# Layer 1's keys and queries by seven block products in place of eight, in a two-layer attention kernel

## The chip, the cores and the metric

The kernel runs on one core of one Trainium2 chip. The metric is the device time of one execution in microseconds (us), lower is better. Of the kernel before there are three timed runs: 2729.54, 2733.97 and 2734.0 us, median 2733.97 us. Beside them stands one execution that was taken with the hardware profiler; every duration below comes from that one.

## What is computed

Two layers work on an image of 2 x 512 channels x 64 x 32, in f32: two batches of 2048 tokens with 512 channels. Layer 0 is an attention with 8 heads of 64, whose keys and queries take an embedding of position beside the channels. Layer 1 is a Nystroem attention with 256 landmarks (each the mean of 8 tokens) and a convolution of the values, and after it a feed-forward map. The part that the change touches is the projection of layer 1's keys and queries and what is read off them at once:

```python
qkv = x @ Wqkv                      # x: normalised tokens, (b, n, 512)
q, k, v = jnp.split(qkv, 3, axis=-1)
q, k, v = (tohead(q), tohead(k), tohead(v))
q = q * scale
qL = q.reshape(b, h, m, l, d).sum(axis=3) / l      # landmarks, l = 8
kL = k.reshape(b, h, m, l, d).sum(axis=3) / l
attn2 = jax.nn.softmax(jnp.einsum('bhid,bhjd->bhij', qL, kL), axis=-1)
```

## The kernel before, in words

Tokens of one batch are held as four blocks of 512 (`NTB = 4`, `TB = 512`); a block is a tile of 128 partitions x 4 chunks of channels x 512 tokens. The 8 heads are worked two at a time, as four **pairs** of each batch; a pair's weight for the keys (or the queries) is a tile of 128 x 4 chunks x 128 columns.

**The unit of the change.** `Pair.keys_and_queries` (from L1231) is a generator. For each of the four token blocks it makes the keys and then the queries: four matmuls (one for each chunk of channels) add up in one PSUM bank (L1244 to L1247), ScalarE copies the bank to SBUF (L1248), SyncE stores the 512 columns in DRAM (L1249), and VectorE takes the sums over 8 tokens (L1250) and the largest absolute value (L1253). That is eight **units** of four matmuls for a pair, with a `yield` after each. After the fourth block L is scaled (L1258), stored, and a few small operations make two bounds from it (L1262 to L1270).

**What stands beside the units.** The engines TensorE, VectorE, ScalarE and GpSimd run their instructions in the order in which the program writes them (`manual_schedule`); only SyncE's DMA queue is ordered by the scheduler. So the interleaving of the generators is the order of the work.

- `Pair.front` of the pair before: `attend` makes the landmark scores on PE (L1286), their exponentials on ScalarE (L1293) and the softmax on VectorE (L1297 to L1303); `gram(0)` and `gram(1)` multiply the softmax by itself (L1313: two banks each, copied out by ScalarE, L1320).
- `others(b, ...)` goes through pairs 1, 2 and 3 of a batch: one unit of the pair, then `attend` of the pair before it, two units, the two `gram`s, and the remaining five units, with a `yield` after each.
- **In batch 0** `others` is advanced by the loop over t (after `drain(out0(0))`) that also finishes layer 0 of batch 1: for each of four token blocks the output projection `out0` (four units of PE, L968, each followed by a VectorE addition, L975, that frees the bank) and the normalisation `norm0_steps`. Its steps are: sums over chunks on VectorE (L986, L987); the mean on PE (L990) and the subtraction on VectorE (L991); the squares on ScalarE (L994, L997) and their sums on VectorE (L1002, L1003); the variance on PE (L1006) and its root on ScalarE (L1008); and, a block later, called as `next(last)`, the reciprocal on VectorE (L1023), the two halves of the multiplication on GpSimd (L1025) and VectorE (L1026), and a DMA issued by GpSimd (L1027).
- **In batch 1** `others` is advanced by a plain loop, and from its eleventh step on each step is followed by one of `second_of_first` (values, landmark attention and convolution of the first pair).

The order of that first loop, for t = 0 to 3:

```python
advance(more)                    # more: others(0, ...)
next(norm)                       # mean, subtraction
advance(more_out or more)        # more_out: out0(t + 1), none at t = 3
if last is not None:
    next(last)                   # reciprocal, multiplication on GpSimd
advance(more_out or more)
next(norm)                       # squares
advance(more, 2 if advance(more_out, 2) else 4)
next(norm)                       # variance, root
```

PSUM has eight banks. In batch 0's stage two of them are the pool behind `bank(...)`, which units, `out0`, the mean, the variance and `gram` all share; `scores_bank` has four, and `values_bank` two that lie idle there. In batch 1's stage `bank(...)` has four and `product_bank` two.

Of the kernel before, what the change touches and what calls it, by code (L numbers as in the profile page):

```python
# [10 lines left out]
F32 = mybir.dt.float32  # L11
I32 = mybir.dt.int32
AF = mybir.ActivationFunctionType
ALU = mybir.AluOpType
AX = mybir.AxisListType

P = 128
B, C, H, W = 2, 512, 64, 32
S = H * W
KC = C // P  # L20
HEADS, D = 8, 64
NPAIR = HEADS // 2
TB = 512
NTB = S // TB
NST = S // P
LM, POOL = 256, S // 256
# [637 lines left out]
def fast_path(  # L664
# [35 lines left out]
    nc = tc.nc  # L700
    dram = ctx.enter_context(tc.tile_pool(name="dram1", bufs=1, space=bass.MemoryType.DRAM))
    const = ctx.enter_context(tc.tile_pool(name="const1", bufs=1))
    small = ctx.enter_context(tc.tile_pool(name="small1", bufs=2))
    banks = ExitStack()
    ps = banks.enter_context(tc.tile_pool(name="ps1", bufs=2, space=bass.MemoryType.PSUM))
    qopool = ctx.enter_context(tc.tile_pool(name="qo1", bufs=NPAIR + 1))
# [4 lines left out]
    kvpool = both.enter_context(tc.tile_pool(name="kv1", bufs=2))  # L711
# [5 lines left out]
    xh_d = dram.tile([B, C, S], F32, name="xh_fd")  # L717
    mT_d = dram.tile([P, KC, C], F32, name="mT_fd")
    k_d = dram.tile([B, NPAIR, P, S], F32, name="k_fd")
    X_d = dram.tile([B, NPAIR, 2, P, 2, LM], F32, name="X_fd")  # L720
    e_d = dram.tile([2, NPAIR, P, S], F32, name="e_fd")
    q_d = dram.tile([B, NPAIR, P, S], F32, name="q_fd")
    o_d = dram.tile([B, NPAIR, P, S], F32, name="o_fd")
    A_d = dram.tile([B, NPAIR, 2, P, 2, LM], F32, name="A_fd")
    L_d = dram.tile([B, NPAIR, P, 2, LM], F32, name="L_fd")
    band_d = dram.tile([HEADS, P * (BAND + 1)], F32, name="band_fd")

    def chunked(ap):
        return ap.rearrange("(k p) n -> p k n", p=P)

    def bank(name):
        return ps.tile([P, 512], F32, tag="pp", name=name)
# [17 lines left out]
    def exps(name):  # L750
        p = ppool.tile([P, 4 * (LM + 1)], F32, tag="p", name=name)
        return p[:, :1024].rearrange("p (h n) -> p h n", h=2)

    def block_of(pool, tag, name):
        return pool.tile([P, KC, TB], F32, tag=tag, name=name)

    def row_of(name):
        return apool.tile([P, TB], F32, tag="rinv", name=name, bufs=3)
# [48 lines left out]
    def drain(gen):  # L807
        for _ in gen:
            pass

    def gap(n=1):
        for _ in range(n):
            yield GAP

    def chain(*gens):
        for g in gens:
            yield from g
# [18 lines left out]
    def load_x(src, b, name, first=0, n=NTB):  # L836
        tiles = []
        for t in range(first, first + n):
            xb = block_of(xpool, "xb", f"{name}_{b}_{t}")
            nc.sync.dma_start(xb, chunked(src[b])[:, :, t * TB : (t + 1) * TB])  # L840
            tiles.append(xb)
        return tiles
# [16 lines left out]
    class Heads0:  # L859


        def __init__(self, b, hp, xbs):
            self.b, self.hp, self.xbs = b, hp, xbs
            self.name = f"f0_{b}_{hp}"
            self.n_units = 13 if b else 15
# [145 lines left out]
    def out0_units(b, t, xb, oTs):  # L1011

        yield from residual_units(b, t, xb, oTs, wo_sb, b0_sb, f"f0_{b}_{t}")
        nc.gpsimd.dma_start(chunked(x1_d[b])[:, :, t * TB : (t + 1) * TB], xb)
# [189 lines left out]
    def write_bands():  # L1204
# [6 lines left out]
        for h in range(HEADS):  # L1211
            nc.sync.dma_start(band_d[h].rearrange("(p q) -> p q", q=BAND + 1), rows[:, h, :])

    class Pair:


# [11 lines left out]
        def begin(self):  # L1228
            self.w = {j: self.load_w(j) for j in (1, 0)}

        def keys_and_queries(self, pool, tag, xhs, after=lambda t: None):  # L1231

            big = small.tile([P, 2, NTB], F32, tag="big", name=f"big_{self.name}", bufs=3)
            most = small.tile([P, 4], F32, tag="most", name=f"most_{self.name}", bufs=3)
            self.L = [
                lmpool.tile([P, LM], F32, tag=f"L{j}", name=f"L{j}_{self.name}") for j in range(2)
            ]
            k = kvpool.tile([P, S], F32, tag="k", name=f"k_{self.name}")
            q = pool.tile([P, S], F32, tag=tag, name=f"q_{self.name}")
            for t in range(NTB):  # L1240
                toks, marks = slice(t * TB, (t + 1) * TB), slice(t * TB // POOL, (t + 1) * TB // POOL)
                for j, dst, dst_d in ((1, k, k_d), (0, q, q_d)):
                    pp = bank(f"pp{j}_{self.name}_{t}")
                    for c in range(KC):  # L1244
                        nc.tensor.matmul(  # L1245
                            pp, lhsT=self.w[j][:, c, :], rhs=xhs[t][:, c, :], start=c == 0, stop=c == KC - 1
                        )  # L1247
                    nc.scalar.copy(dst[:, toks], pp)  # L1248
                    nc.sync.dma_start(dst_d[self.b, self.hp][:, toks], dst[:, toks])  # L1249
                    nc.vector.tensor_reduce(  # L1250
                        self.L[j][:, marks], dst[:, toks].rearrange("p (m l) -> p m l", l=POOL), AX.X, ALU.add
                    )
                    nc.vector.tensor_reduce(  # L1253
                        big[:, j, t : t + 1], dst[:, toks], AX.X, ALU.max, apply_absolute_value=True
                    )
                    if t == NTB - 1:
                        L = self.L[j]
                        nc.vector.tensor_scalar(L, L, (1.0, D**-0.5)[j == 0] / POOL, None, ALU.mult)  # L1258
                        nc.sync.dma_start(L_d[self.b, self.hp][:, j, :], L)
                    yield  # L1260
                after(t)
            nc.vector.tensor_reduce(most[:, :2], big, AX.X, ALU.max)  # L1262
            for j in range(2):
                nc.vector.tensor_reduce(
                    most[:, 2 + j : 3 + j], self.L[j], AX.X, ALU.max, apply_absolute_value=True
                )

            c = B * NPAIR + 2 * self.i
            nc.vector.tensor_tensor(bound[:, c : c + 1], most[:, 2:3], most[:, 1:2], ALU.mult)
            nc.vector.scalar_tensor_tensor(  # L1270
                bound[:, c + 1 : c + 2], most[:, :1], D**-0.5, most[:, 3:], ALU.mult, ALU.mult
            )
# [447 lines left out]
    todo = [(b, hp) for b in range(B) for hp in range(NPAIR)]  # L1720
# [4 lines left out]
    for n, (b, hp) in enumerate(todo[:-1]):  # L1725
# [5 lines left out]
        if finish is None:  # L1731
            units = nxt.units(wait=nb - b)
        else:

            units = nxt.units(False, lambda: outs_done)
# [20 lines left out]
    lmpool = both.enter_context(tc.tile_pool(name="lm1", bufs=2))  # L1756
# [4 lines left out]
    pairs = [[Pair(b, hp) for hp in range(NPAIR)] for b in range(B)]  # L1761
    xhs = load_x(xh_d, 0, "xh")
    pairs[0][0].begin()
    units = chain(gap(2), pairs[0][0].keys_and_queries(qopool, "qo", xhs))
# [3 lines left out]
    def beside(main, other):  # L1768

        for n in main:  # L1770
            yield
            for _ in range(n):
                if next(other, other) is other:
                    break
                yield

    def others(b, xhs, last, after=lambda t: None):

        for hp in range(1, NPAIR):
            pair = pairs[b][hp]  # L1780
            pair.begin()
            units = pair.keys_and_queries(kvpool, "k", xhs, after if hp + 1 == NPAIR else lambda t: None)
            next(units)
            yield
            yield from beside(last.front(), units)
            yield from units
            last = pair


    next_xhs, over = [], False  # L1790

    def load_next(t):
        assert over
        next_xhs.extend(load_x(xh_d, 1, "xh", t, 1))

    more = [others(0, xhs, pairs[0][0], load_next)]
    b = B - 1

    def as_block(tile):
# [8 lines left out]
    def norm0(t):  # L1808
        part = apool.tile([P, 2, TB], F32, tag="acc", name=f"part_f0_{t}")
        return norm0_steps(b, t, xbs_[t % 2], xns_[t % 2], part)  # L1810

    def out0(t):
        xb = xbs_[t % 2]
        nc.sync.dma_start(xb, chunked(x[b])[:, :, t * TB : (t + 1) * TB])
        return out0_units(b, t, xb, oTs)

    drain(out0(0))
    last, norm = None, norm0(0)
    next(norm)
    for t in range(NTB):  # L1820
# [12 lines left out]
        last = norm  # L1833
# [19 lines left out]

    xhs = next_xhs
    pairs[1][0].begin()
    units = pairs[1][0].keys_and_queries(kvpool, "k", xhs)
    next(units)
    drain(beside(pairs[0][-1].front(), units))
    drain(units)
    todo = pairs[1] + pairs[0]  # L1860
# [16 lines left out]
    def second_of_first():  # L1877
        pair = todo[0]
        yield from values(0)
        yield from pair.attn3()  # L1880
        landmarks, start, conv = pair.landmarks_values(), pair.start_values(), convolution(0)
        for part in (landmarks, conv, landmarks, start, conv):
            next(part)
            yield
        drain(conv)
        next(start)
        yield
# [5 lines left out]

    xhs_of = [xhs]
    first = second_of_first()
    for i, _ in enumerate(others(1, xhs, todo[0])):
        if i == 8:
            todo[0].prefetch_w()
            todo[0].prefetch()
        if i >= 10:  # L1900
            next(first, None)
# [27 lines left out]
    for n, pair in enumerate(todo):  # L1929
        before = todo[n - 1] if n else None  # L1930
        after = todo[n + 1] if n + 1 < len(todo) else None
# [18 lines left out]
        if n:  # L1950
            q = late_buffer if n > NPAIR + 1 else lambda name: kvpool.tile([P, S], F32, tag="k", name=name)
# [236 lines left out]
```

## Time and profile before

| | |
|---|---|
| timed runs | 2729.54, 2733.97, 2734.0 us (median 2733.97) |
| span of the profiled execution | 2730.4 us (its own time is not listed apart; the span lies between the lowest and the highest run, 3.6 us under the median) |
| TensorE (PE) busy | 2688.2 us, 98% of the span |
| VectorE (DVE) / ScalarE (ACT) / GpSimd (POOL) busy | 1628.1 / 903.7 / 161.8 us |
| matmuls of layer 1's keys and queries, L1245 | 512 records, 227.8 us of PE |
| stage of batch 0, 1401.9 to 1555.1 us: PE, DVE, POOL busy | 149.0, 103.3, 20.0 of 153.2 us |
| stage of batch 1, 1555.1 to 1721.3 us: PE, DVE, POOL busy | 166.2, 75.2, 0.0 of 166.2 us |

How to read it: an f32 matmul leaves two records on PE, each with a weight load of its own (PEld) that lies beside the matmul before it. The mean of one record (597 ns) is longer than the distance from one record to the next (0.43 us), because records overlap in the pipeline; the distance is what a matmul costs. A group's idle time, with the engine and line that ended it, is the time in which the engine had nothing to run just before that group. The two stages run from the end of `drain(out0(0))` to the `attend` of batch 0's last pair, and from there to that of batch 1's last pair.

### The profile page before, as it was taken

What the parts mean: (1) busy time and instruction counts of PE and PEld (TensorE: products, weight loads), DVE (VectorE), ACT (ScalarE), POOL (GpSimd) and SP (SyncE); (2) the same over time, 40 slices, a digit from 0 to 9 for tenths busy, and PEclk for the clock granted to TensorE, in tenths of its full rate; (3) what the DMA queues carried; (4) which work ended last, traced back from release to release, by engine and by line L of the source; (5) the groups of instructions that cost most, each with busy time, mean ns of one, the idle gap of its engine ahead of it and who ended that gap; (6) DMA issues with size and microseconds to landing.
All of it is one profiled execution on the core that took longest, in us unless ns stands there. A gap on an engine that the chain in (4) does not pass through costs nothing.

```text
span 2730.4 us, 41173 instructions
## 1 busy us (share of the span) xinstructions
PE 2688.2 (98%) x16994; PEld 1361.7 (50%) x16994; DVE 1628.1 (60%) x2087; ACT 903.7 (33%) x1352; POOL 161.8 (6%) x109
## 2 busy tenths in 40 slices
PE   9999999999999999999999999999999999999999
PEld 5343443434443334344344455777677666655344
DVE  3768777664557765656667544445544645465565
ACT  1434343434334334444422223223323222231210
POOL 0101101000001100000002000000000000000000
PEclk9999999999999999999999999999999999999999
DMA  4100000212111200012024632312212112121211
GB/s 147 43 10 24 28 21 24 86 36 70 32 65 56 97 24 21 24 40 77 24 89 167 207 120 93 103 33 90 79 37 63 59 44 97 34 71 42 89 39 48
DMA packets 111476, 173.99 MB, mean 64 GB/s; under 512 B 16176, under 2 KB 67888, under 8 KB 106672
## 3 DMA queue, kind: packets, MB, share of 16 engines
q1 hardware_dynamic: 105136, 150.00, 17.0%
q0 software_dynamic: 5440, 20.97, 2.1%
q8 instruction: 135, 2.21, 0.3%
q14 instruction: 61, 0.50, 0.1%
q10 hardware_dynamic: 704, 0.31, 0.0%
HBM read 90.87 MB, written 63.57 MB: 57 GB/s over the span
## 4 chain that ended last, share of the span: by engine, by line
PE 90%; DVE 5%; DMA 1%; SPq 1%; ACT 1%; issue 1%; POOL 0%; DVEq 0%; ACTq 0%; POOLq 0%
PE sc_f L1072 15%; PE av_f L1102 15%; PE pp L1245 8%; PE pb L1538 5%; PE pa L1538 5%; PE vp_f L953 4%; PE vp L953 4%; PE pp_k_f L905 4%; PE yp_g L968 4%; PE yp_f L968 4%; PE fp_g L1694 3%; PE pp_q_f L905 3%; PE sc L1367 2%; PE sc L1595 2%; PE av L1611 2%; PE av L1388 2%
## 5 line engine op out<-in xcount | busy, mean ns | idle before, releaser
L1090 DVE TENSOR_TENSOR acc_f<-acc_f,p_f 128x1024 f32<-128x1024 f32 x448 | 581.0, 1297 | 209.5 <-ACT p_f L1080 181.0
L1080 ACT ACTIVATE p_f<-sc_f 128x1024 f32<-128x1024 f32 x512 | 496.4, 1021 | 564.2 <-PE sc_f L1072 561.5
L1072 PE MATMUL sc_f<-q_f,k_f 64*64 64x512 f32 x4096 | 491.2, 595 | 2.7 <-ACT p_f L1080 2.7
L1102 PE MATMUL av_f<-p_f,v_f 64*64 64x512 f32 x4096 | 484.3, 589 | 0.0
L1102 PEld LDWEIGHTS av_f<-p_f,v_f 64*64 64x64 f32 x4096 | 156.6, 133 | 283.0 <-issue 283.0
L1072 PEld LDWEIGHTS sc_f<-q_f,k_f 64*64 64x64 f32 x4096 | 145.8, 133 | 285.6 <-issue 261.9
L1245 PE MATMUL pp<-xh,w 128*128 128x512 f32 x512 | 227.8, 597 | 0.7 <-ACT q L1248 0.7
L1538 PE MATMUL pa<-M 128*128 128x192 f32 (+1 forms) x640 | 153.2, 385 | 6.3 <-ACT M L1529 6.3
L1245 PEld LDWEIGHTS pp<-xh,w 128*128 128x128 f32 x512 | 94.8, 190 | 119.6 <-issue 113.0
L1538 PE MATMUL pb<-R 128*128 128x192 f32 (+1 forms) x640 | 149.3, 380 | 0.5 <-DVE M L1551 0.5
L1538 PEld LDWEIGHTS pa<-M 128*128 128x128 f32 x640 | 109.3, 195 | 27.8 <-ACT M L1529 9.4
L953 PEld LDWEIGHTS vp_f<-wv_f,x 128*128 128x128 f32 x1024 | 115.7, 192 | 13.5 <-issue 11.8
L953 PE MATMUL vp<-w,xh 128*128 128x128 f32 x1024 | 120.9, 277 | 0.0
L953 PEld LDWEIGHTS vp<-w,xh 128*128 128x128 f32 x1024 | 117.0, 192 | 7.2 <-issue 4.6
L953 PE MATMUL vp_f<-wv_f,x 128*128 128x128 f32 x1024 | 118.8, 277 | 0.0
L1538 PEld LDWEIGHTS pb<-R 128*128 128x128 f32 x640 | 106.5, 190 | 23.6 <-DVE M L1551 0.8
L905 PE MATMUL pp_q_f<-x,wq_f 128*128 128x512 f32 x256 | 114.2, 598 | 1.7 <-DMA x<-in_x_dram 1.2
L905 PE MATMUL pp_k_f<-x,wk_f 128*128 128x512 f32 x256 | 114.3, 599 | 1.5 <-DVE k_f L908 1.1
L968 PE MATMUL yp_g<-o,wo_f 128*128 128x512 f32 x256 | 114.8, 597 | 0.0
L968 PE MATMUL yp_f<-q_f,wo_f 128*128 128x512 f32 x256 | 113.6, 598 | 0.9 <-DVE xr_f L975 0.9
L1120 POOL TENSOR_TENSOR q_f<-q_f,rinv_f 128x512 f32<-128x512 f32 x32 | 45.6, 1426 | 1040.1 <-DMA rinv_f<-acc_f 785.4
L1694 PE MATMUL fp_g<-xn_g,mT 128*128 128x512 f32 (+1 forms) x232 | 99.8, 580 | 0.0
(210 smaller groups left out, 2718.7 us busy)
## 6 DMA issues: line engine op xcount, KB each, us to landing
xh<-xh_fd SPq DMA_DIRECT2D x12, 1024.0 KB, 5.5
rinv_f<-acc_f SPq DMA_DIRECT2D x256, 32.0 KB, 1.9
xr_f<-in_x_dram SPq DMA_DIRECT2D x8, 1024.0 KB, 5.3
x_fd<-xr_f POOLq DMA_DIRECT2D x8, 1024.0 KB, 4.8
xh_fd<-xn_f POOLq DMA_DIRECT2D x8, 1024.0 KB, 4.8
k_fd<-k SPq DMA_DIRECT2D x32, 256.0 KB, 2.8
q_fd<-q SPq DMA_DIRECT2D x32, 256.0 KB, 2.8
k<-k_fd SPq DMA_DIRECT2D x8, 1024.0 KB, 6.4
```

The source lines that it names most:

```text
L905: nc.tensor.matmul(pp, lhsT=w_sb[kind][:, k, cols], rhs=xbs[t][:, k, :], start=k == 0, stop=k == KC - 1)
L953: nc.tensor.matmul(vp[:, j * P : (j + 1) * P], lhsT=xb[:, k, j * P : (j + 1) * P], rhs=w_of(k), start=k == 0, stop=k == KC - 1,)
L968: nc.tensor.matmul(yp, lhsT=wo_sb[:, k, m * P : (m + 1) * P], rhs=oTs[k][:, toks], start=k == 0, stop=k == NPAIR - 1,)
L1072: nc.tensor.matmul(sc[r * D : (r + 1) * D, h, :], lhsT=hd.k[rows, lo : lo + D], rhs=hd.q[rows, t * TB : (t + 1) * TB], start=True, stop=True,)
L1080: nc.scalar.activation(p, sc, AF.Exp, scale=D**-0.5)
L1090: nc.vector.tensor_tensor(acc, first if c == 1 else acc, p, ALU.add)
L1102: nc.tensor.matmul(av[r][half, :], lhsT=hd.v[keys, c, half], rhs=pp[keys, h, :], start=c == 0, stop=c == NST - 1,)
L1245: nc.tensor.matmul(pp, lhsT=self.w[j][:, c, :], rhs=xhs[t][:, c, :], start=c == 0, stop=c == KC - 1)
L1367: nc.tensor.matmul(scs[h][:, j * LM : (j + 1) * LM], lhsT=self.k[rows, c * P : (c + 1) * P], rhs=self.L[0][rows, :], start=True, stop=True,)
L1388: nc.tensor.matmul(self.av3[half, :LM], lhsT=self.v[:, c, half], rhs=self.p3[s][:, h, j * LM : (j + 1) * LM], start=c == 0, stop=c == NST - 1,
L1538: nc.tensor.matmul(dst, lhsT=lhsT[:, k, t * P : (t + 1) * P], rhs=rhs[:, k, :], start=k == 0, stop=k == 1)
L1694: nc.tensor.matmul(fp[:, cols], lhsT=mT[:, k, m * P : (m + 1) * P], rhs=self.xn[:, k, cols], start=k == 0, stop=k == KC - 1,)
```

## The change

Two token blocks x0 and x1 and the two halves of the channels (`lo`: chunks 0 and 1, `hi`: chunks 2 and 3) make keys and queries a 2 x 2 by 2 x 2 product of blocks. Winograd's form of Strassen's scheme needs seven block products for it in place of eight. A **product** here is two matmuls (two chunks) of 512 columns. Pairs 1, 2 and 3 of both batches are changed; pair 0 keeps `keys_and_queries`.

- `Combined.make` prepares four sums of token blocks for two blocks at a time (VectorE, 128 x 1024 each), once for each batch: 16 operations. In batch 0 two of them follow each of the four units of `out0(0)`; in batch 1 one follows each of the eight units of pair 0.
- `combine_w` prepares four sums of weights for each pair on GpSimd (128 x 256 each), emitted after a pair's second product; the third product reads the second of them.
- `seven_products` makes a pair in two units of seven products. Bank `u` (from `values_bank` or `product_bank`) takes products 1, 6, 7 and 4 one on top of the other, and ScalarE copies its contents out after each of the four. Product 2 has a `bank(...)` of its own. Product 5 opens a second one (`pb`), VectorE adds its contents to one result, product 3 is added to the same bank, and VectorE adds that to another result.
- The 14 products are emitted in an order written by hand; the last two of a pair (the *tail*) come after the first product of the next pair. `stored` is what L1249 to L1259 did, but now for 1024 tokens at a time.
- The weights of the next pair are loaded in the middle of a pair (`halfway`) and not at its beginning; batch 1's token blocks are loaded two at a time.

```diff
+        def make(self):
...
+            t1, t2, t3, t4 = self.room(x1[:, lo, :])
+            nc.vector.tensor_tensor(t1, x1[:, lo, :], x0[:, lo, :], ALU.subtract)
+            yield
+            nc.vector.tensor_tensor(t3, x1[:, hi, :], x1[:, lo, :], ALU.subtract)
+            yield
+            nc.vector.tensor_tensor(t2, x1[:, hi, :], t1, ALU.subtract)
+            yield
+            nc.vector.tensor_tensor(t4, x0[:, hi, :], t2, ALU.subtract)
...
+        def combine_w(self):
...
+            for out, a, b, op in (
+                (s1, wq[:, lo, :], wq[:, hi, :], ALU.add),
+                (s2, s1, wk[:, lo, :], ALU.subtract),
+                (wq[:, lo, :], wk[:, lo, :], wq[:, lo, :], ALU.subtract),
+                (s4, wk[:, hi, :], s2, ALU.subtract),
+            ):
+                nc.gpsimd.tensor_tensor(out, a, b, op)
+            self.ws |= {3: s4, 4: wq[:, hi, :], 5: s1, 6: s2, 7: wq[:, lo, :]}
...
+                def product(to, m, start=True):
+                    for k in range(2):
+                        nc.tensor.matmul(
+                            to, lhsT=self.ws[m][:, k, :], rhs=part.of[m][:, k, :],
+                            start=start and k == 0, stop=k == 1, skip_group_check=True,
+                        )
...
+                u = chain_bank(f"pu_{name}")
+                product(u, 1)
+                nc.scalar.copy(d[:, 0, 0, :], u)
+                yield
+                pp = bank(f"pc_{name}")
+                product(pp, 2)
+                add(0, 0, pp)
+                yield
+                product(u, 6, False)
+                nc.scalar.copy(d[:, 0, 1, :], u)
+                yield
+                pp = bank(f"pb_{name}")
+                product(pp, 5)
+                yield
+                product(u, 7, False)
+                nc.scalar.copy(d[:, 1, 1, :], u)
+                add(1, 1, pp)
+                yield
+                product(u, 4, False)
+                nc.scalar.copy(d[:, 1, 0, :], u)
+                done(0)
+                yield
+                product(pp, 3, False)
+                add(0, 1, pp)
+                done(1)
+                yield
+
+            units = [unit(tp, part) for tp, part in enumerate(parts)]
+            for n, i in enumerate("00000100111111"):
+                next(units[int(i)])
+                if n == 1:
+                    self.combine_w()
+                if n == 8:
+                    halfway()
+                if n == 13:
+                    self.end_landmarks()
+                yield
...
-    def others(b, xhs, last, after=lambda t: None):
-
+    def others(b, parts, last, chain_bank, after=lambda tp: None):
...
+        tail = None
+        pairs[b][1].begin()
         for hp in range(1, NPAIR):
...
+            units = pairs[b][hp].seven_products(parts, chain_bank, halfway)
+            turn(units, 1)
+            if tail:
+                turn(tail)
+            yield
+            for n in last.front():
+                yield
+                if n:
+                    turn(units, n + 1)
+                    yield
+            for _ in range(4):
+                turn(units)
+                yield
+            tail, last = units, pairs[b][hp]
+        turn(tail)
+        yield
+        after(1)
...
-    drain(out0(0))
+    for _ in out0(0):
+        next(making)
+        next(making)
+    drain(making)
```

`turn(gen, n=2)` advances a generator n times; `done(j)` calls `stored` for 1024 tokens of the queries (0) or the keys (1); `add` is a VectorE addition of a bank and an SBUF row of 512.

## Prediction

> **What bounds the kernel now.** I read the busy shares first, then the costliest groups, then the two stages by windows, then PE's order of time in them.
>
> ```profile
> PE 2688.2 (98%) x16994; PEld 1361.7 (50%) x16994; DVE 1628.1 (60%) x2087; ACT 903.7 (33%) x1352; POOL 161.8 (6%) x109
> ...
> L1245 PE MATMUL pp<-xh,w 128*128 128x512 f32 x512 | 227.8, 597 | 0.7 <-ACT q L1248 0.7
> ```
>
> PE is the bound, and the units of keys and queries hardly wait (0.7 us in 512 records). The windows of the two stages (length, then PE, PEld, DVE, ACT and POOL busy, granted clock, DMA):
>
> ```profile
> 1401.90:1555.10 153.20, 149.00 (x387) 67.36 (x385) 103.27 (x146) 36.73 (x58) 20.00 (x15) 1.00 0.53 178
> 1555.10:1721.30 166.20, 166.20 (x741) 92.72 (x740) 75.22 (x151) 42.82 (x84) 0.00 (x0) 1.00 0.34 113
> ```
>
> In batch 0's stage PE waits 4.2 us in four places, in batch 1's nowhere. But DVE is busy two thirds of the first, in bursts, and these show in PE's order of time:
>
> ```profile
> 1486.09 1.14 PE L1286 MATMUL sc<-L,L 64*128 64x256 f32 x8
> 1487.16 7.13 PE L1245 MATMUL pp<-xh,w 128*128 128x512 f32 x16
> 1496.14 1.55 PE L1313 MATMUL pr<-X 128*128 128x257 f32 x8 [1.85 <-DVE X L1299]
> 1497.71 1.12 PE L1006 MATMUL var_n<-xr_f,mean_w 128*128 128x512 f32 x2
> 1498.68 1.03 PE L1313 MATMUL pr<-X 128*128 128x257 f32 x4
> 1500.94 0.71 PE L1313 MATMUL pr<-X 128*128 128x129 f32 x4 [1.24 <-ACT rstd_n L1008]
> ```
>
> Even with 7 us of units between `attend` and `gram`, DVE came 1.85 us late. The same stretch holds the rows that price the new waits, DVE's and GpSimd's:
>
> ```profile
> 1440.17 2.71 DVE L1002 TENSOR_TENSOR xr_f<-xr_f 128x1024 f32<-128x1024 f32 x1
> ...
> 1480.13 2.28 DVE L991 TENSOR_TENSOR xn_f<-xr_f,mean_n 128x2048 f32<-128x2048 f32 x1
> ...
> 1484.50 3.35 DVE L1023 RECIPROCAL rstd_n<-rstd_n 128x512 f32<-128x512 f32 x1
> ```
> ```profile
> 1488.00 3.32 POOL L1025 TENSOR_TENSOR xn_f<-xn_f,rstd_n 128x1024 f32<-128x1024 f32 x1 [19.32 <-DVE rstd_n L1023]
> 1491.61 0.79 POOL L1027 DMA_DIRECT2D xh_fd<-xn_f  x1 [0.30 <-POOL xn_f L1025]
> ```
>
> **What is saved.** 16 records are 7.13 us with a pipeline tail, 0.43 us from one to the next. A changed pair has 56 records in place of 64: 8 x 0.43 = 3.44 us. Six pairs: 20.6 us, three in each batch. This is certain; the question is what waits.
>
> **Costs that lie beside PE.** Per pair: ScalarE's copies stay eight (0.58 us). DVE's reductions cover the same columns (512 of them stand 0.60 apart, so 1.2 for 1024) and six additions from PSUM come on top (0.69 us as L1109): 4 us of DVE in 24 us of PE, under PE's cover; without that cover 4 us a pair. A copy after a product of `u` (0.1 + 0.58 us, and 0.1 back) hides behind the next product of 1.72 us wherever another stands between two products of `u`; only batch 0's last pair (and batch 1's, behind other work) has 7 and 4 back to back: 0.9 us. On SP's queue, stores become four of 1024 tokens in place of eight; the weights' loads move to the middle of the pair before, five products (8.6 us) ahead of their use, and land in 3.3 us; batch 1's last two blocks (5.5 us each) are issued later, but some 19 us before their use: nothing, and at most one landing, 5.5 us, if they queue behind other transfers. Batch 1's `Combined` (8 x 1.22 us of DVE over eight units of 3.44 us) hides as well.
>
> **New waits, batch 0.** I write the instructions in program order on each engine and start each when its engine, its input and its bank are free. Turns of `others` are numbered; a pair takes nine: (1) product 1 and the tail of the pair before; (2) `attend`; (3) products 2, 6, 5 and `combine_w`; (4), (5) `gram`; (6) 7, 1'; (7) 4, 3; (8) 2', 6'; (9) 5', 7' (a prime is the second unit).
>
> a. *First mean.* The eight sums of `Combined` (1.22 each) sit between `out0(0)`'s additions; the last two come after the last addition and delay L986/L987 by 2.4 us, while PE's cover before the mean shrinks from 3.44 to 1.72. Wait 3.6 us; GpSimd's first `combine_w` falls there too, and L1002 took 2.71 us beside GpSimd's L1025 against 1.22 alone, so up to 6.8. I take **5**. The first variance then finds its bank 0.9 late.
>
> b. *The bank held.* `pb` is taken in turn 3 and let go after product 3 in turn 7. The pool has two banks, so for that long all others share one, and each evacuation stands in PE's way. For pair 1 this lasts from t = 0 to t = 2: the bank of the variance (ScalarE's table load 1.28 and root 0.69 first) 2.1; after each of the `gram` banks a copy, 0.6 + 0.5 + 1.0 + 0.6; the mean's bank until L991 ends, 2.4; `out0`'s four banks, an addition each (0.2 + 0.75), one of them behind the reciprocal and its multiplication, 1.0 + 1.9 + 1.0: **11**. At t = 2 DVE's 1024-wide reductions delay the mean's subtraction: **2.5**. Pairs 2 and 3: `gram` on one bank, 1.7 each, and pair 3's first waits 2.0 more for the addition that frees product 2's bank behind `attend`'s DVE work: **5.4**.
>
> c. *Landmarks late.* Before, a unit of the next pair (3.44 us) lay between the last unit and `attend`. Now products 4' and 3' end just before it. From the start S of 4': copied at S + 2.4, two reductions and scaling to S + 5.05, addition 0.69, two reductions 2.4, scaling 0.2: the landmarks are ready at S + 8.4. PE ends 3' at S + 3.4; for pair 1 a mean (0.86) follows: 4.1; for pair 2 nothing: 5.0; for pair 3 the next unit, 1.5: **10.6**.
>
> d. *Weight sums behind a normalisation.* At t = 3 the order is turn 1 of pair 2, mean, turn 2, `next(last)`, turn 3. So GpSimd's `combine_w` of pair 2 stands behind L1025 and L1027, and these behind DVE's reciprocal, which stands behind `attend`'s softmax and, before it, the mean's subtraction. From S: landmarks 8.4, small operations 9.4, subtraction 2.28 to 11.7, two softmaxes (2.2 each, as L1297 to L1303) 16.1, reciprocal 19.5, L1025 22.9, its DMA issue 24.0, two sums of weights 25.6. No row has 128 x 256 on GpSimd; 128 x 512 takes 1.27 to 1.78 us, so one of these lies between half (0.64) and that (1.78); I take 0.8, near half of the mean 1.43. PE reaches product 6 at S + 11.2: **14.5** (14.2 to 16.5). What is queued behind it on PE is all of pair 2. In the other pairs GpSimd is free in time.
>
> Sum: 5.9 + 11 + 2.5 + 5.4 + 10.6 + 14.5 + 0.9 = 50.8 us. Of the 4.2 us waited now nothing stays apart from it.
>
> **New waits, batch 1.** `bank` has four here, GpSimd nothing else to do, so only c remains: pair 1 0.7 (its predecessor keeps the old units, 1.72 us of cover against 2.4), pair 2 4.8, pair 3 2.8 (a step of landmark attention, 2.1, in between), the last pair none: 8.3 us.
>
> **Sum.** Batch 0: 50.8 - 4.2 - 10.3 = +36.3; the same order laid out on the clock, where waits overlap a little, puts `attend` of pair 3 at 1588.3 in place of 1555.07: +33.2. I take +35. Batch 1: 8.3 - 10.3 = -2. Together +33: span 2730.4 + 33 = 2763. The median of the runs is 3.6 above the span: **2767 us**.
>
> [...] The granted clock is 1.00 in both stages, and PE's longest wait there is 1.85 us, so no run here shows what PE does after a longer gap. [...]
>
> **Rivals.**
> 1. *The side engines keep ahead* (not slower). The place is the queues of DVE and GpSimd: were their work always emitted early enough for PE, waits would stay at today's 4.2, and the span would be 2730.4 - 20.6 = 2710, a run 2713; with the 15 us of a and batch 0's c left, 2728. For it: PE is 98% busy, DVE 60%. Against it: the 1.85 us wait above, behind more cover than a to d leave. It decides where PE's new waits sum to less than 20.6 us.
> 2. *Only part of the waits.* The weight sums come early (d is gone), or the bank is free (b is gone): 2767 - 14.5 = 2752, or 2767 - 19 = 2748; with c halved in both batches as well (9.5) 2739. For it: GpSimd is busy 20 us in the stage; it needs an order other than the one I counted.
> [...]
> 4. *It doesn't save records.* 56 for 64 is written out; I give it no chance.
>
> **How the numbers follow.** My forecast, 2752 to 2792 around 2767, has 0.66; rival 2 (2739 to 2752) 0.16; rival 1 0.08; a balance within 0.2% (5.5 us, about what a measurement of this kernel tells from none) 0.05; rival 3 0.05. Slower: 0.66 + 0.16 + 0.05 = 0.87. The range takes the forecast and rival 2, rounded: 2738 to 2792.
>
> **What would show it.** L1245's records and those of the products together: 512 - 48 = 464, some 20 us less PE. PE's waits in batch 0's stage near 50 us: one near 14 on GpSimd before the second pair's product 6; three of 1.5 to 5 on DVE before L1286; waits of about 1 us before L968 on L975, none of which are there now. In batch 1 two or three before L1286. If the first is missing, d is wrong; if L968 doesn't wait, b is wrong; then rival 2 holds.

## The result, and the profile after

The changed kernel takes 2779.68 us (median of four runs, 2777.93 to 2780.93), the kernel before 2733.98 us beside it (2729.54 to 2734.2): 1.0171 times as long, 95% interval 1.0157 to 1.0186. The profiled execution took 2780.93 us, its span is 2779.0 (before 2730.4), 48.6 us more. The page's line of busy time:

```profile
PE 2689.9 (97%) x16946; PEld 1360.9 (49%) x16946; DVE 1670.1 (60%) x2091; ACT 904.5 (33%) x1352; POOL 182.9 (7%) x133
```

PE has 16946 records in place of 16994: the 48 are gone. Yet its busy time has not fallen. The windows of the two stages (length, then PE, PEld, DVE, ACT, POOL busy, granted clock, DMA share, GB/s), with the same boundaries in the program as before, tell why:

```profile
1402.04:1601.32 199.28, 153.99 (x362) 67.23 (x360) 116.22 (x143) 36.98 (x58) 30.39 (x24) 0.90 0.40 138
1601.32:1771.85 170.53, 162.28 (x718) 91.92 (x717) 93.83 (x153) 42.84 (x84) 9.41 (x15) 0.96 0.35 118
```

Batch 0's stage is 46.1 us longer (153.20 before), batch 1's 4.3 longer (166.20), everything else together 1.8 shorter. The granted clock (the clock that TensorE was given, as a share of full speed) was 1.00 in both stages and is now 0.90 and 0.96. PE's waits from 1400 to 1800 us (total, times, longest), the eight largest:

```profile
PE sc L1394 <- DVE L L1365: 16.2, 4, 4.9
PE pu L1298 <- POOL s L1281: 12.3, 1, 12.3
PE mean_n L990 <- DVE part_f L987: 5.4, 1, 5.4
PE pr L1421 <- ACT A L1428: 3.5, 8, 0.5
PE yp_f L968 <- DVE xn_f L991: 3.3, 2, 2.4
PE yp_f L968 <- DVE xr_f L975: 3.2, 3, 1.5
PE pp L1261 <- issue: 2.2, 1, 2.2
PE pr L1421 <- ACT rstd_n L1008: 2.1, 1, 2.1
```

In the changed code L1298 is a product (`pu`, `pc`, `pb`: its bank), L1394 the landmark scores, L1365 the scaling of the landmarks, L1281 `combine_w` on GpSimd, L1308 the addition from PSUM, L1421 `gram`, L1261 a unit of pair 0 in the old form. Waits of the mean, of the scores, on the weight sums and of `out0` (L968) are all there. And PE's order of time shows what stands behind a wait:

```profile
1409.35 2.07 PE L990 MATMUL mean_n<-part_f,mean_w 128*128 128x512 f32 x2 [5.43 <-DVE part_f L987]
1411.22 15.89 PE L968 MATMUL yp_f<-q_f,wo_f 128*128 128x512 f32 x32
...
1444.79 5.95 PE L968 MATMUL yp_f<-q_f,wo_f 128*128 128x512 f32 x8 [2.38 <-DVE xn_f L991]
...
1527.58 3.78 PE L1298 MATMUL pu<-t_first,s 128*128 128x512 f32 x4 [12.32 <-POOL s L1281]
```

The mean's two records take 2.07 us, and 1.02 where nothing was waited for; 32 records of `out0` 15.89 in place of 13.90; four of a product 3.78 in place of 1.88. The windows around these places have a granted clock of one half:

```profile
1409.30:1413.50 4.20, 4.15 (x5) 1.85 (x6) 1.98 (x1) 0.00 (x0) 0.58 (x1) 0.50 0.00 0
1444.70:1449.00 4.30, 4.21 (x5) 1.83 (x6) 0.03 (x1) 2.00 (x2) 0.00 (x0) 0.50 0.00 0
...
1723.00:1728.00 5.00, 5.00 (x22) 2.93 (x24) 4.11 (x12) 1.09 (x2) 0.00 (x0) 0.50 0.08 26
```

So the 46.1 and 4.3 us by which the two stages are longer come out of three terms. The waits are summed from PE's order of time; the last term is what is left of a stage's length when the others are taken off.

| us | batch 0 | batch 1 |
|---|---|---|
| stage before | 153.2 | 166.2 |
| 24 records fewer | -10.3 | -10.3 |
| waits, after less before | 45.3 - 4.1 = +41.2 | +8.3 |
| left: slower records after waits | +15.2 | +6.4 |
| stage after | 199.3 | 170.5 |

### The profile page after: what moved, and what is told of

Same layout as the page of the kernel before. It is cut to its first block, busy times and chain, and to the rows that moved or that the text cites. A ratio compares the mean times of both kernels' runs of the same rounds, so it can differ in the third digit from the quotient of the medians.

```text
span 2779.0 us, 41074 instructions
## 1 busy us (share of the span) xinstructions
PE 2689.9 (97%) x16946; PEld 1360.9 (49%) x16946; DVE 1670.1 (60%) x2091; ACT 904.5 (33%) x1352; POOL 182.9 (7%) x133
## 4 chain that ended last, share of the span: by engine, by line
PE 89%; DVE 6%; ACT 1%; DMA 1%; issue 1%; SPq 1%; POOL 0%; DVEq 0%; ACTq 0%; POOLq 0%
PE sc_f L1072 15%; PE av_f L1102 15%; PE pa L1646 5%; PE pb L1646 5%; PE vp L953 4%; PE vp_f L953 4%; PE pp_k_f L905 4%; PE fp_g L1802 4%; PE yp_g L968 4%; PE yp_f L968 3%; PE pp_q_f L905 3%; PE pu L1298 3%; PE sc L1703 2%; PE sc L1475 2%; PE av L1496 2%; PE pp L1261 2%
## 5 line engine op out<-in xcount | busy, mean ns | idle before, releaser
L968 PE MATMUL yp_f<-q_f,wo_f 128*128 128x512 f32 x256 | 118.8, 617 | 8.4 <-DVE xr_f L975 4.0
L953 PEld LDWEIGHTS vp_f<-wv_f,x 128*128 128x128 f32 x1024 | 115.7, 192 | 13.5 <-issue 11.8
L968 PE MATMUL yp_g<-o,wo_f 128*128 128x512 f32 x256 | 114.8, 597 | 0.0
L1740 POOL TENSOR_TENSOR o<-o,rinv 128x512 f32<-128x512 f32 x32 | 46.3, 1446 | 815.3 <-DVE rinv L1739 586.3
L1708 ACT ACTIVATE p<-sc 128x512 f32<-128x512 f32 x128 | 66.6, 601 | 93.4 <-PE sc L1703 93.1
```

What stands on the lines that cost most here:

```text
L953: nc.tensor.matmul(vp[:, j * P : (j + 1) * P], lhsT=xb[:, k, j * P : (j + 1) * P], rhs=w_of(k), start=k == 0, stop=k == KC - 1,)
L968: nc.tensor.matmul(yp, lhsT=wo_sb[:, k, m * P : (m + 1) * P], rhs=oTs[k][:, toks], start=k == 0, stop=k == NPAIR - 1,)
L1708: nc.scalar.activation(p[:, h, :], sc, AF.Exp, scale=D**-0.5)
```

## The experiments

The theory after the result: four separate losses in batch 0 (the token sums ahead of the first mean, the held bank, the late landmarks, the weight sums behind a normalisation), one in batch 1 (the late landmarks), and a half clock behind each. The rivals: a wait that is taken away comes back in the next place, since DVE, GpSimd and ScalarE serve all of them; or the seven products cost more than they save even without waits. Diffs are against the changed kernel; times are medians, with the ratio to the kernel before, which took 2732.3 to 2733.5 us (medians) beside them.

### Weight sums one product earlier

```diff
-                if n == 1:
+                if n == 0:
                     self.combine_w()
```

> Only change against the changed kernel (2779.7 us): the four sums of weights of a pair are emitted after its first product and not after its second, so that GpSimd has those of pair 2 of batch 0 before the normalisation's multiplication. Theory (the sum of waits a to d, each followed by a stretch of half clock): the wait of 12.3 us on GpSimd before product 6 goes, and the half clock behind it (about 2 us); but the bank of product 2 is freed by a VectorE addition that stands behind the reciprocal, so gram waits some 5 to 6 us in its place: 7 to 9 us less, 2771 to 2773. Rival (VectorE's queue is one chain that PE follows whatever GpSimd does): the wait moves whole to the next VectorE result, 2777 to 2780. A third reading (the wait is simply gone): 14 less, 2766.

2771.73 us, 1.0143 (1.0126 to 1.0160), 8.0 less, the theory's number. GpSimd's sums now stand ahead of its normalisation, and the wait of 12.32 us is gone. A part of it comes back two products later, where the same normalisation on DVE holds up product 2's addition, and with it the bank that `gram` needs, as PE's order of time in this run shows:

```profile
1510.05 2.09 PE L1394 MATMUL sc<-L,L 64*128 64x256 f32 x8 [3.86 <-DVE L L1365]
...
1522.83 2.08 PE L1421 MATMUL pr<-X 128*128 128x257 f32 x4 [4.74 <-DVE kq L1308]
```

The agreement is in part chance. In the profiled execution batch 0's stage is only 5.2 us shorter (194.1); another 2.8 come from batch 1, whose waits are the same (8.2 us) but whose records behind the longest of them, 4.72 us, are shorter: the scores and the 32 records after them take 6.58 us (1.83 and 4.75) in place of 8.04 (2.08 and 5.96).

### A bank of its own for products 5 and 3 in batch 0

```diff
-                pp = bank(f"pb_{name}")
+                pp = bank(f"pb_{name}") if self.b else scores_bank(f"pb_{name}")[:, 0, :]
```

> Only change against the changed kernel (2779.7 us): in batch 0 product 5's bank, which is held until product 3 is out, is taken from the scores banks, so that the two banks of the common pool serve the others. Theory: the waits of out0, gram, mean and pc on an evacuation go, 14.6 us by the changed kernel's trace, and the half clock around 1440 to 1449 us, 3 us: 13 to 18 less, 2762 to 2767. Rival (VectorE is late there anyway, banks or not): the waits on evacuations turn into waits on sums and landmarks, 5 or less to be had, 2775 to 2780.

2761.61 us, 1.0109 (1.0092 to 1.0126), 18.1 less: the largest of the losses. PE's waits in this run (from 1400 to 1800 us), the fourth to the sixth of the eight lines:

```profile
PE yp_f L968 <- DVE xn_f L991: 2.2, 1, 2.2
PE pp L1261 <- issue: 2.2, 1, 2.2
PE pr L1421 <- ACT rstd_n L1008: 1.2, 1, 1.2
```

The 3.5 us on L1428, the 3.2 on L975 and the small ones on L1308 are gone, and batch 0's waits fall from 45.3 to 32.7: 12.7 us. The other 5.4 go to slow records that no longer follow them (batch 0's stage is 18.0 us shorter in the profiled execution, 181.3): the second `out0`, 5.95 + 3.70 us for its first 16 records before, now takes 13.90 for all 32.

### Half of the token sums a block later

Part 1's four operations stand beside `out0(1)` (t = 0), after the first mean.

```diff
-    for _ in out0(0):
-        next(making)
-        next(making)
-    drain(making)
+    for m, _ in enumerate(out0(0)):
+        if m < 2:
+            next(making)
+            next(making)
...
```

> Only change against the changed kernel (2779.7 us): of batch 0's eight sums of token blocks the last four are emitted beside the next block's output projection and not before the first mean. Theory: the wait of 5.4 us before the first mean and 2.7 us of half clock after it go: 7 to 8 less, 2772 to 2773. Rival (GpSimd's sums of weights at the same time hold VectorE up, not its own four operations): 2 to 3 less, 2777.

2774.63 us, 1.0155 (1.0138 to 1.0172), 5.1 less, between the two expectations. The first mean's wait falls from 5.4 to 1.5, and the slow `out0` behind it is at 13.9 again.

### PE kept busy while it waits

Six, four, five and eleven matmuls whose result nothing reads stand in PE's order ahead of the first mean, of the scores of two pairs, and of pair 2's product 6; the computation is otherwise unchanged.

```diff
+        def fill(self, n, name):
+            if self.b == 0:
+                idle = scores_bank(f"{name}_{self.name}")[:, 0, :]
+                for _ in range(n):
+                    nc.tensor.matmul(idle, lhsT=mean_w, rhs=xhs[2][:, 0, :], start=True, stop=True)
...
```

> The changed kernel (2779.7 us) with matmuls into a bank that nobody reads, put into PE's queue ahead of four waits of batch 0: 6 before the first mean, 4 and 5 before the landmark scores of pairs 1 and 2, 11 before product 6 of pair 2, each lot shorter than the wait it stands in. They add work and take no wait away. Theory that what follows a wait is dear because PE's clock has been halved: the stretches after these waits run at full clock, 6 to 9 us less, 2771 to 2774. Rival (the records after a wait are long for another reason, such as late weight loads): no change, 2779 to 2781, or some more.

2775.30 us, 1.0150 (1.0133 to 1.0168), 4.4 less, between the two expectations, but the four runs lie apart (2769.87, 2771.63, 2778.97, 2779.51; the profiled one is the last), so the sum is weak evidence. The granted clock over the whole profiled execution is 0.992 in place of 0.989, while the filling, 26 matmuls of two records of 0.43 us, takes 2 us more than the 20.2 us of waits that it stands in. The single places are clearer. PE's order of time:

```profile
1410.81 1.12 PE L990 MATMUL mean_n<-part_f,mean_w 128*128 128x512 f32 x2 [0.28 <-DVE part_f L987]
1411.77 13.90 PE L968 MATMUL yp_f<-q_f,wo_f 128*128 128x512 f32 x32
...
1510.26 1.14 PE L1402 MATMUL sc<-L,L 64*128 64x256 f32 x8 [0.42 <-DVE L L1373]
...
1527.28 3.51 PE L1304 MATMUL pu<-t_first,s 128*128 128x512 f32 x4 [4.53 <-POOL s L1281]
```

(L1304 is the product and L1402 the scores here.) The mean starts when DVE allows it, 1.5 us later than without the filling, but it and the `out0` behind it go at full speed: 1.12 and 13.90 in place of 2.07 and 15.89, the scores 1.14 in place of 1.90. The last line is the counter-example in the same run: eleven matmuls did not cover the wait on GpSimd, 4.53 us of idle PE remained, and the product behind them took 3.51 in place of 1.88. So slow records came after idle time here whichever engine had ended it: DVE ahead of the 2.07 us of the mean in the changed kernel, GpSimd ahead of these 3.51.

### Another order in batch 1

Turns in `others`: product 1 and the tail; 2, 6, 5; 7, 1'; scores; 4, 3; 2', 6'; `gram`, `gram`; 5', 7'.

```diff
+            if b:
+                turn(units, 3)
+                yield
+                turn(units)
+                yield
+                for n in last.front():
+                    yield
+                    if n:
+                        for _ in range(n):
+                            turn(units)
+                            yield
+                turn(units)
+                yield
+            else:
...
```

> Against the changed kernel (2779.7 us) only batch 1's order within a pair is another: products 2, 6, 5, 7 and 1' come before the landmark scores of the pair before, and 4, 3, 2', 6' between them and gram. So 8.6 us of products lie between the tail and the scores in place of none. In batch 1 neither banks nor GpSimd are short, so this tells of the late landmarks alone (c). Theory: the waits of 0.8, 4.7 and 2.7 us before the scores go, and the half clock after two of them (6 us): 2765 to 2767. Rival (the softmax then comes late for gram, and the wait moves there): half of it or less, 2772 to 2780.

2766.22 us, 1.0126 (1.0109 to 1.0143), 13.5 less, as expected: 8.3 of waits and the slow records behind them.

### Seven products in batch 1 alone

Batch 0 keeps the old units and old loads (`others` as in the kernel before); batch 1 is as changed.

```diff
-    more = [others(0, parts, pairs[0][0], values_bank, load_next)]
+    more = [others_by_eight(0, xhs, pairs[0][0], load_next)]
...
```

> Seven products in batch 1 alone, in the changed kernel's own order; batch 0 has the old eight units. Theory: batch 1 gives 10.3 us of matmuls and takes 8.2 us of waits and 6 us of half clock: 4 us over the kernel before (2732.5 here), 2736 to 2738. Rival (batch 1's part is free of harm and all of the loss is batch 0's): 2722. Other rival (both batches share the loss): 2750 to 2758.

2734.88 us (ten runs), 1.0009 (1.0000 to 1.0019): 2.1 us over the kernel before: without batch 0's disturbances, too, batch 1 gains nothing as it stands. In its profiled execution (span 2730.0, 0.4 under the kernel before) 10.3 are saved, 8.0 are waited before the scores, and 1.6 of the 1.9 left are the slower records behind the wait of 4.72 us: the scores and the 32 records after them take 6.58 us in place of 4.98 (granted clock 0.59 from 1618.0 to 1621.4 us). (This execution is the fastest of the ten.) The changed kernel has 13.7 us of half clock behind the same waits; 6 us of loss by it had been expected here.

### Batch 1 alone, with the other order

The two edits above together.

> As the run with seven products in batch 1 alone, with the other order of this pair's products and scores there. Theory: no wait is left in batch 1, and the saving of 24 records of 0.43 us is all that is left: 10.3 us under the kernel before (2732.5), 2721 to 2724. Rival (seven products cost something beside waits, such as copies or accumulation on a bank that is being read): 2726 or more.

2722.87 us, 0.9965 (0.9951 to 0.9979): 9.9 us under the kernel before, close to the 10.3 of the records. PE's waits from 1555 to 1760 us in this run are one line, a wait that belongs to the landmark attention:

```profile
PE sc L1475 <- DVE M L1659: 0.7, 3, 0.2
```

The products themselves therefore cost next to nothing beyond their records where nothing waits: 0.4 us by the medians, 0.8 by batch 1's stage in the profiled execution (156.7 us where 166.2 - 10.3 = 155.9 were due). The second rival falls.

### All four together, with the other order in both batches

The edits of the weight sums, the bank, the token sums and the order (now for both batches); one more product ahead of the first mean, and at t = 3 the last normalisation's second half a turn later.

```diff
-        advance(more)
+        advance(more, 1 if t else 2)
...
-        if last is not None:
+        if last is not None and t + 1 < NTB:
             next(last)
...
+        if t + 1 == NTB:
+            next(last)
         next(norm)
```

> All four waits taken away at once, in both batches: the sums of weights after the first product (d), product 5's bank from the scores banks (b), the last sums of token blocks beside the next output projection and one more turn of products before the first mean (a), the order with products between tail and scores (c), and at t = 3 the last normalisation's reciprocal and multiplication moved behind the products of that round. Theory: 20.6 us are saved and some 3 us of waits stay at the end of batch 0: 2714 to 2718, faster than the kernel before (2732.5). Rival (batch 0's stage has become VectorE's: 116 us busy of 153, in one order): waits of 10 us or more come back elsewhere there, 2722 to 2735.

2740.21 us (nine runs), 1.0027 (1.0017 to 1.0037): 22 us over the top of my expectation, and above the rival's too. Batch 1 has no such wait left; batch 0 has 21 us of them, the largest:

```profile
PE pu L1298 <- POOL s L1281: 5.1, 2, 4.7
PE sc L1394 <- ACT X L1401: 3.8, 3, 1.6
PE yp_f L968 <- DVE xn_f L991: 2.9, 1, 2.9
```

Pair 3's weight sums now stand behind the last normalisation on GpSimd, and the scores wait for ScalarE's exponentials: by the code they come while products 5 and 3 hold one of the scores' four banks, so that they must wait for another one. No run separates this.

### The same without the extra product

> All four losses undone as in the run that gave 2740, without the extra product ahead of the first mean. Theory 1, the extra product only moves 1.7 us of PE: 2738 to 2742, the wait for the first mean back at 3 to 5 us and another one shorter by as much. Theory 2, the shift that it gave the whole order by half a turn is what set pair 3's weight sums behind the last normalisation (4.7 us waited there): 2732 to 2736, with that wait gone.

2741.84 us, 1.0034 (1.0022 to 1.0047): the first theory's number, but not its reason, since the first mean's wait came back at 1.5 us only. The wait on GpSimd is indeed gone, which was the second theory's sign, but 9.9 us are now waited before the scores on L1401 and 6.3 at one place on the variance's root (L1008). Neither theory had these two. What this run and the one before share is the other order in batch 0.

### Three losses undone, the other order in batch 1 alone

> The weight sums a product earlier, the bank of its own, part 1's sums a block later, and the other order in batch 1 alone; batch 0 keeps its order. Theory 1, the four losses stand apart and add up: the gains measured one by one, 8.0 + 18.1 + 5.1 + 13.5 = 44.7 us, are taken off 2779.7, 2733 to 2738, and then the other order in batch 0, which stood beside them in the run of all four (2740), was worth nothing or less there. Theory 2, they share DVE, GpSimd and ScalarE in batch 0, so a wait that goes comes back in the next place: 10 us or more of the 44.7 are missing, 2745 to 2755, and the other order in batch 0 was worth what is missing beyond 2740.

2731.24 us (ten runs), 0.9993 (0.9984 to 1.0003): 48.4 us less than the changed kernel, where the four single gains add up to 44.7; that is 1.8 under the first theory's range. In the profiled executions batch 0's stage is 35.2 us shorter, where the three changes alone make it 5.2, 18.0 and 7.3 shorter, 30.5 together, and batch 1's is 13.9 shorter, as with the other order alone. So no gain is lost when the others are there, though the sums agree only within some 5 us; and the other order, with the last normalisation's later turn, was a loss of 9 to 11 us in batch 0. What is left there, before the scores:

```profile
1490.93 2.08 PE L1394 MATMUL sc<-L,L 64*128 64x256 f32 x8 [3.86 <-DVE L L1365]
...
1529.20 2.09 PE L1394 MATMUL sc<-L,L 64*128 64x256 f32 x8 [4.75 <-DVE L L1365]
```

These are the late landmarks, unchanged, with the slow records (2.08 for eight that take 1.14).

### Two products ahead of the scores in batch 0

On top of the last one: products 2 and 6 come before the scores of the pair before, and product 1' fills their place after them. The bank that 5 and 3 hold is still taken after the scores.

```diff
             turn(units, 1)
             if tail:
                 turn(tail)
+            if not b:
+                turn(units)
             yield
...
-                for _ in range(4):
-                    turn(units)
+                for n in (1, 1, 2, 2):
+                    turn(units, n)
                     yield
```

> The run that gave 2731.24 (three losses undone, the other order in batch 1), and in batch 0 products 2 and 6 come before the scores of the pair before in place of after them, product 1' takes their place between scores and gram. Theory 1, the landmarks then have 3.4 us more of PE's work as cover: of the waits before the scores, 3.9 and 4.8 us, 0.4 and 1.3 stay, the half clock after them and the 1.5 us before the first mean go, 7 us and some 4 of half clock less, 2719 to 2725, about as the version with batch 1 alone (2722.9) or faster. Theory 2, what DVE and GpSimd are late with comes back one place on (gram on the softmax, or pair 3's product 6 on the weight sums, which end at 1527 where that product now comes): half of it at most, 2726 to 2731.

2721.84 us, 0.9963 (0.9949 to 0.9977): the fastest, 10.8 us under the kernel before. The page's busy time and the window of batch 0's stage, for the lines at the head of the prediction:

```profile
PE 2668.6 (98%) x16946; PEld 1353.5 (50%) x16946; DVE 1668.8 (61%) x2091; ACT 903.5 (33%) x1352; POOL 178.4 (7%) x133
```
```profile
1402.36:1555.53 153.17, 138.80 (x361) 62.88 (x359) 117.64 (x144) 36.49 (x58) 28.47 (x24) 1.00 0.51 179
```

PE's busy time is 19.6 us under that of the kernel before: the 20.6 saved are seen at last. But batch 0's stage has the length that it had (153.2): the 10 us that the records save are waited elsewhere, in 14 gaps of 14.2 us in all (4.1 before), none of them above 2.43, and the clock is 1.00. The version with batch 1 alone is at 2722.87, so seven products in batch 0 bring nothing that can be told from no change, even in the best order tried.

## Why the prediction was right, point by point

The predicted time is 12.7 us low of the result and the result lies in the range. The mechanism, records saved and more than lost to new waits in batch 0, is shown by the runs that take the waits away one by one. The sum came out by two errors that partly cancel: 5.5 us of waits too many, and 21.6 us of slow records left out. Without the first the result would lie further off; that it lies well inside the range is in part the width of the range.

- *Saved, 20.6.* Right: 128 + 336 = 464 records of units and products, and 19.6 us less PE in the last run, where the clock is 1.00 in both stages.
- *a, 5 + 0.9.* Measured 5.43 and 0.54.
- *b, 11 + 2.5 + 5.4 = 18.9.* The place is right; as waits it is over-sized: 12.7 go with a bank of its own. The 18.1 us that the run gains are those and 5.4 of slow records, so the agreement with 18.9 is chance. Some waits that I gave to the bank stay without it: 1.25 us on the variance's root and 2.22 on the mean's subtraction, which are DVE's and ScalarE's own lateness.
- *c, 4.1 + 5.0 + 1.5 and 0.7 + 4.8 + 2.8.* Measured 3.86 and 4.88 in batch 0; 0.80, 4.72 and 2.73 in batch 1. The 1.5 before the last pair's scores did not come; 2.19 us before batch 1's first unit did, with no releaser in the profile. Nearest to it in time is that pair's second weight load (in the last run it is issued at 1548.1 and lands 3.1 us later, 0.8 before the unit starts at 1551.9), but no run was made to show it.
- *d, 14.5.* Measured 12.32, by the chain that was counted: GpSimd's order of time has the normalisation at 1521.57, its DMA issue, and then

```profile
1525.99 0.74 POOL L1281 TENSOR_TENSOR s<-w 128x256 f32<-128x256 f32 x1
1526.81 0.72 POOL L1281 TENSOR_TENSOR s<-s,w 128x256 f32<-128x256 f32 x1
```

  with 0.8 taken for what measures 0.74 and 0.72. The chain was right to 0.3 us: the sums that product 6 reads were ready 25.3 us after product 4' began (25.6 counted). The wait is shorter because PE came later, 13.0 us after that start in place of 11.2: the scores and product 2 before it ran at half clock (1.90 and 2.87 us in place of 1.14 and 1.88). What the price left out is that it does not come back whole: undoing it gains 8.0 us, of which 5.2 lie in batch 0's stage, because DVE is nearly as late as GpSimd at that place.
- *0.9 for product 4 after 7.* Measured 0.7. *Costs beside PE:* no wait on stores or token blocks is seen, unless the 2.19 above is one.
- *The term that was mis-sized: PE's speed after a wait.* The sum had it at nothing: in the kernel before, PE's longest wait in the two stages was 1.85 us, at a granted clock of 1.00. It measures 15.2 + 6.4 = 21.6 us. All five gaps of 3.86 us or more in the changed kernel were followed by a granted clock of 0.50, but so were a gap of 2.73 us and a row of shorter ones from 1435 to 1440 us; the stretch at half clock behind that row lasted 10.24 us, and a gap of 2.38 fell into it. By the trace's record of the granted clock the half-speed stretches fill 41.0 us of batch 0's stage and 13.7 of batch 1's; PE was idle for 15.4 and 0.9 of that, and the rest at half speed loses (41.0 - 15.4) / 2 = 12.8 and 6.4 us. That leaves 2.4 of the 21.6 without a name. The last section shows which gaps do this.
- *Rivals.* Rival 1's price, 2713 to 2728, is what an order without the waits reaches in fact (2721.84 and 2722.87); its condition, new waits under 20.6 us, holds there (10.0) and not in the changed kernel (49.5). Rival 2 fell: all of a to d were there. Rival 3 had 0.05, for a time over 2792: PE was slow behind the waits, by 21.6 us, but the time is 12 us under that.

What stays open: why the other order costs what it does in batch 0 (the waits are named above, but only the order as a whole was taken out), and whether the 14.2 us of waits left there can be got rid of.

## What to carry to other kernels

Where the bound engine is 98% busy, price an edit that saves it work by what the others must have ready at each point in program order, and count a gap by its length and by the slow records that can stand behind it too (here 21.6 us of them beside 49.5 of new waits). A bank that is held across other work in a pool of two was the dearest part here, 18 us for the 10 that the stage could save. And before such a change is dropped, make it alone where the side engines have room, in an order that puts work between a result and its reader: that turned +46 us into -10.

## What the runs showed of the hardware

- In the changed kernel's trace the stretches at a granted clock of one half last 6.83, 10.24, 3.41, 13.65 and 6.83 us in batch 0's stage and 6.83 twice in batch 1's, all multiples of 3.41, and so are the stretches at full clock between them (23.89, 61.44, 3.41, 30.72, 95.57 and 51.20). Half clock went with how long PE had been idle within one such step of 3.41 us, not with how long the gap was. The two stages, cut into these steps, have seven at full clock with 2.05 us of idle or more, and each of the seven stretches at half clock stands behind one of them; no other step at full clock there has more than 1.58. The runs give no limit between the two: a step with 1.57 us was followed by half clock in the run of all four (1496.40 to 1499.82), one with 1.62 by full clock in the last run (1452.44 to 1455.85). The same wait before the same scores, 2.73 us, shows it. In the changed kernel 2.17 of it fall into one step, and in the run with batch 1 alone it is split 1.11 and 1.62. The windows are set on the steps (length, PE busy first; the clock is the third number from the right); the step and the two after it in the changed kernel:

```profile
1719.03:1722.44 3.41, 1.24 (x10) 0.69 (x8) 3.38 (x5) 1.08 (x2) 0.00 (x0) 1.00 0.79 313
1722.44:1729.27 6.83, 6.27 (x25) 3.58 (x26) 5.87 (x17) 1.33 (x3) 0.00 (x0) 0.50 0.16 55
```

  and the two steps in the run with batch 1 alone, at full clock, as is the step after them (1.00):

```profile
1669.81:1673.22 3.41, 2.30 (x17) 1.17 (x16) 3.38 (x5) 1.08 (x2) 0.00 (x0) 1.00 0.78 286
1673.22:1676.63 3.41, 1.79 (x16) 1.25 (x16) 3.41 (x9) 0.66 (x3) 0.00 (x0) 1.00 0.41 157
```

  In the same way 2.43 us in the last run (1.62 and 0.80) and 2.87 us in the run of all four (1.46 and 1.41) were followed by full clock, and several short waits that add up to 2.05 us in one step (1435.72 to 1439.14, changed kernel) were followed by the half-speed stretch of 10.24 us. The steps were read from the traces, and no run shifted a gap against them on purpose.
- What a gap cost behind it differed from run to run. Behind the same wait of 4.72 us before the scores of batch 1, the scores and the 32 records after them took 8.04 us in the changed kernel, 6.58 in the run with the weight sums earlier, 6.60 in the one with the bank of its own and 6.58 in the one with batch 1 alone (4.98 in the last run, where nothing was waited for). Behind the wait of 2.73 us, the scores and the 16 records after them took 6.13 us in the changed kernel, 5.00 with the bank of its own and 3.35 with batch 1 alone. That fits runs which lie up to 9.6 us apart (2769.87 to 2779.51 with the filling), though their single traces were not compared.
- An addition of 128 x 256 on GpSimd took 0.72 us with DVE idle (at 1526.81 us in the changed kernel) and up to 1.70 where DVE's additions ran beside it (at 1407.05; DVE's own addition of L986 took 1.74 us there and 1.21 at 1501.10).
